# A fourth tile for the weighted values, two tiles for the output, and two steps written in other slices, in a kernel of dilated attention and a binary convolution

## The chip, the core and the metric

The kernel runs on one core of a Trainium2 chip. Its time is the device time of the core in microseconds (us); three runs are given with their median. Besides these there is one profiled execution, whose trace tells when every instruction of every engine started and ended. The engines are called as the profile calls them: PE does the matrix multiplications (PEld is its loading of weights), DVE is VectorE, ACT is ScalarE, POOL is GpSimd, SP is SyncE, which issues most of the DMAs.

## The reference, cut to what matters

The input is an image batch `x` of 16 x 56 x 56 x 384 in float32. There are two layers, each with a residual.

```python
# layer 0: attention over 9 dilated neighbours, three groups of 128 channels
x = x + attention(_gn(x), w_qkv, w_proj, b_proj)
# layer 1: depthwise 3x3 convolution with the signs of w
x = x + conv(_gn(x), sign(clip(w)))

def _gn(v, G=32, eps=1e-5):          # over a whole image and 12 channels
    g = v.reshape(B_, H_, W_, G, C_ // G)
    return (g - mean(g)) / sqrt(var(g) + eps)

def _dilate_attention(q, k, v, head_dim, kernel, dil):   # per group, dil = 1, 2, 3
    attn = einsum('bgdn,bgdkn->bgnk', q, unfold(k)) * head_dim ** -0.5
    attn = softmax(attn, axis=-1)                         # over the 9 neighbours
    return einsum('bgnk,bgdkn->bgnd', attn, unfold(v))
```

Each group has 4 heads of 32 channels, so a pixel has 3 x 4 x 9 = 108 attention weights. The output of layer 0 is projected with `w_proj`.

## The kernel before, in words

Channels lie on the partitions, three groups `j` or `g` of 128. An image is cut into 7 chunks of 8 rows (448 pixels), so there are 112 chunks `m`. The work of all chunks is cut into small pieces; `at(when, order, piece)` files a piece under a slice of time and an order in this slice, and at the end all pieces are emitted in that order. A chunk begins every 9 slices (`STEP = 9`). Written order is not the last word: the framework that builds the program plans each engine's queue itself, from the written order and from when it thinks that inputs and tiles will be there.[...]

What a chunk goes through, with `t0 = 9 m`:

- Stage A (`plan_a`, 12 or more chunks ahead): the pixels are turned so that channels lie on partitions (L423), copied out (L435), `bn_stats` gathers the statistics of layer 0 (L436), and the chunk goes to DRAM.
- Stage B, slices `t0 - 14` to `t0 + 26`: PE projects q, k and v (L464). DVE multiplies q with k for three neighbours at a time into a tile `t` of 128 x 1344 (L517), PE sums over the channels of a head (L502) into the scores `ps`. In slices `t0 + 9` to `t0 + 12` comes the softmax: ACT copies the scores (L534), PE turns them (L537), DVE takes maxima, sums and the quotient (L540 to L548), ACT rounds the weights to bfloat16 (L556), GpSimd subtracts (L560, `softmax_4`), rounds the rest (L564) and subtracts again (L565), so that each weight is three bfloat16 terms. SP then issues a transposing DMA of them into `aT` (L570).
- Weighing (`weigh(i)`, i = 0 to 8, slices `t0 + 14 + i`): PE spreads three neighbours' weights over the channels (L583) into the PSUM tile `pb_a`, of which there is one. DVE multiplies it with v into a tile `w` of 128 x 1344 (L590). In a group of three, with `ky` = 0, 1, 2, GpSimd adds the second and the third `w` to the first (L598, twice) and then sums the three neighbours in it to `y` (L601, L602). PE projects `y` (L616), DVE adds the residual (L619) and gathers the statistics of layer 1 (L622).
- Stage C (`plan_c`, 10 chunks later): two groups are convolved on PE from normalised tiles `z` (L697, L711), the third with ACT's products (L762), which GpSimd adds (L768, L773, L776). PE turns the result (L783), ACT copies it to a tile `osb` (L788), SP issues the DMA to the output (L791). The last image goes other ways: its `z_last` uses tiles of `t` and `w`, its `osb_last` tiles of `y`.

Between images stands `group_norm`, filed by `statistics` as six steps: `channels` (L310, three `bn_aggr` of DVE per set of statistics), `mean`, `deviation`, `variance`, `invert` and `spread_out`, in slices 0, 1, 2, 4, 5 and 7 after `when`. In the middle of the run one call serves layer 1 of image b and layer 0 of image b + 2.

Tiles come from pools. `w_p` has 3 tiles of `w` (L151), `o_p` 3 of `osb` (L158). A pool gives out the tile that has been free for the longest, and an instruction that writes it waits for the last one that used it. With three tiles of `w` this makes the multiplication L590 wait as follows: for `ky` = 0 for the first addition (L598) of the group before, for `ky` = 1 for the second addition of the group before, for `ky` = 2 for its last sum to `y` (L602). A tile `w` goes 5376 bytes into each partition, an `osb` 1536, `rest` 2048.

Of the kernel before, what the change touches and what calls it, by code (L numbers as in the profile page):

```python
# [8 lines left out]
F32 = mybir.dt.float32  # L9
# [8 lines left out]
P = 128  # L18
HEADS = 4
HD = 32  # L20
NG = 3
# [3 lines left out]
SUB = 112  # L25
# [3 lines left out]
NPAD = 32  # L29
# [6 lines left out]
def dilated_attention_then_binary_conv(  # L36
# [28 lines left out]
    nc = tc.nc  # L65
    B, H, W, C = x.shape
    PX = ROWS * W
    NCH = H // ROWS
    NSUB = PX // SUB
# [12 lines left out]
    of = out.rearrange("b h w c -> b (h w) c")  # L82
# [63 lines left out]
    st_p = ctx.enter_context(tc.tile_pool(name="st_p", bufs=2))  # L146
# [1 line left out]
    xn_p = ctx.enter_context(tc.tile_pool(name="xn_p", bufs=3))  # L148
    xr_p = ctx.enter_context(tc.tile_pool(name="xr_p", bufs=1))
    t_p = ctx.enter_context(tc.tile_pool(name="t_p", bufs=4))  # L150
    w_p = ctx.enter_context(tc.tile_pool(name="w_p", bufs=3))  # L151
    y_p = ctx.enter_context(tc.tile_pool(name="y_p", bufs=4))
    s_p = ctx.enter_context(tc.tile_pool(name="s_p", bufs=1))
    a_p = ctx.enter_context(tc.tile_pool(name="a_p", bufs=2))
    x1_p = ctx.enter_context(tc.tile_pool(name="x1_p", bufs=2))
    xg_p = ctx.enter_context(tc.tile_pool(name="xg_p", bufs=2))
    m_p = ctx.enter_context(tc.tile_pool(name="m_p", bufs=3))
    o_p = ctx.enter_context(tc.tile_pool(name="o_p", bufs=3))  # L158


    kv = []
# [134 lines left out]
    def group_norm(sets):  # L296

        had = {}
        L = len(sets)

        def channels():
            had["ch"] = ch = st_p.tile([P, L, NG, 2], F32, tag=f"ch{L}", name="ch")
            for n, (stats, _, _) in enumerate(sets):
                for j in range(NG):
                    nc.vector.bn_aggr(ch[:, n, j, :], stats[:, j].rearrange("p c s -> p (c s)"))  # L310

        def mean():
            had["pair"] = pair = st_p.tile([GN_G, L, 3], F32, tag=f"pair{L}", name="pair")
            pm = ps_mt.tile([P, 512], F32, tag="mt", name="pm")
            for j in range(NG):
                nc.tensor.matmul(
                    pm[:GN_G, 0:L], gsel[:, j], had["ch"][:, :, j, 0], start=(j == 0), stop=(j == NG - 1)
                )
            nc.vector.tensor_scalar_mul(pair[:, :, 2], pm[:GN_G, 0:L], -1.0 / GN_CH)

        def deviation():

            ch = had["ch"]
            pb = ps_mt.tile([P, 512], F32, tag="mt", name="pb")
            for j in range(NG):
                nc.tensor.matmul(
                    pb[:, j * L : (j + 1) * L], gselT[:, j], had["pair"][:, :, 2], start=True, stop=True
                )
            had["dev"] = dev = st_p.tile([P, L, NG], F32, tag=f"dev{L}", name="dev")
            nc.vector.tensor_tensor(  # L330
                dev, pb[:, : NG * L].rearrange("p (j l) -> p l j", l=L), ch[:, :, :, 0], ALU.add
            )
            nc.gpsimd.tensor_tensor(dev, dev, dev, ALU.mult)
            nc.gpsimd.tensor_tensor(dev, dev, ch[:, :, :, 1], ALU.add)

        def variance():
            dev = had["dev"]
            pv = ps_mt.tile([P, 512], F32, tag="mt", name="pv")
            for j in range(NG):
                nc.tensor.matmul(pv[:GN_G, 0:L], gsel[:, j], dev[:, :, j], start=(j == 0), stop=(j == NG - 1))  # L340
            had["var"] = var = st_p.tile([GN_G, 3, L], F32, tag=f"var{L}", name="var")
            v, r = var[:, 0], var[:, 1]
            nc.vector.tensor_scalar(v, pv[:GN_G, 0:L], 1.0 / GN_CH, 1e-5, op0=ALU.mult, op1=ALU.add)

            ri = r.bitcast(I32)
            nc.vector.tensor_single_scalar(ri, v.bitcast(I32), 1, op=ALU.arith_shift_right)
            nc.vector.tensor_scalar(ri, ri, -1, RSQRT_BITS, op0=ALU.mult, op1=ALU.add)

        def invert():

            var, pair = had["var"], had["pair"]
            v, r, t = var[:, 0], var[:, 1], var[:, 2]
            for step in range(3):
                nc.gpsimd.tensor_tensor(t, r, r, ALU.mult)
                nc.gpsimd.tensor_tensor(t, t, v, ALU.mult)
                nc.gpsimd.tensor_scalar(t, t, -0.5, 1.5, op0=ALU.mult, op1=ALU.add)
                nc.gpsimd.tensor_tensor(pair[:, :, 1] if step == 2 else r, r, t, ALU.mult)
            nc.gpsimd.tensor_tensor(pair[:, :, 0], pair[:, :, 2], pair[:, :, 1], ALU.mult)

        def spread_out():  # L360
            pair = had["pair"]
            pp = ps_mt.tile([P, 512], F32, tag="mt", name="pp")
            for j in range(NG):
                nc.tensor.matmul(
                    pp[:, 2 * L * j : 2 * L * (j + 1)], gselT[:, j], pair[:, :, 0:2], start=True, stop=True
                )
            mr = st_p.tile([P, NG, L, 2], F32, tag=f"mr{L}", name="mr", bufs=5 - L)
            nc.vector.tensor_copy(mr.rearrange("p j l s -> p (j l s)"), pp[:, : 2 * L * NG])
            for n, (_, done, for_convolution) in enumerate(sets):
                if not for_convolution:  # L370
                    done(mr[:, :, n])
                    continue

                pz = ps_mt.tile([P, 512], F32, tag="mt", name="pz")
                for s in range(JG * NQ):
                    of_set = gselT[:, s // NQ, s % NQ * HD : s % NQ * HD + HD]
                    for ky in range(3):
                        nc.tensor.matmul(
                            pz[ky * HD : (ky + 1) * HD, 2 * s : 2 * s + 2], of_set, pair[:, n, 0:2],
                            start=True, stop=True,  # L380
                        )
                mrz = st_p.tile([K3, JG, NQ, 2], F32, tag="mrz", name="mrz")
                nc.vector.tensor_copy(mrz.rearrange("p j q s -> p (j q s)"), pz[:K3, : 2 * JG * NQ])
                done(mr[:, :, n], mrz)

        return channels, mean, deviation, variance, invert, spread_out

    def chunk_of(dram, c):
# [4 lines left out]
    def at(when, order, piece):  # L393

        pieces.setdefault((when, order), []).append(piece)

    stats0, stats1 = {}, {}
    xd, x1d = {}, {}
    mr0, mr1 = {}, {}
# [46 lines left out]
    def plan_b(m, t0):  # L446

        b, c = divmod(m, NCH)
        had = {}
# [75 lines left out]
        def by_neighbour(ap):  # L525
            return ap.rearrange("p s (o k) -> p s o k", o=NTAP)

        def over_neighbours(ap):
            return ap.unsqueeze(2).to_broadcast([SUB, NSUB, NTAP, GH])

        def softmax_1():

            sT = s_p.tile([P, PX], F32, tag="sT", name="sT")
            nc.scalar.copy(sT, had.pop("ps")[:, :PX])  # L534
            pt = ps_mt.tile([P, 512], F32, tag="mt", name="pt_s")
            for s in range(NSUB):
                nc.tensor.transpose(pt[:SUB, s * P : (s + 1) * P], sT[:, s * SUB : (s + 1) * SUB], permf)  # L537
            pt4 = pt[:SUB].rearrange("p (s v) -> p s v", s=NSUB)[:, :, :NR]
            mx = s_p.tile([SUB, NSUB, GH], F32, tag="mx", name="mx")
            nc.vector.reduce_max(mx, by_neighbour(pt4).rearrange("p s o k -> p s k o"), axis=AX.X)  # L540
            nc.vector.tensor_tensor(by_neighbour(weights), by_neighbour(pt4), over_neighbours(mx), ALU.subtract)
            nc.scalar.activation(weights, weights, AF.Exp, scale=SCALE)
# [13 lines left out]
            nc.scalar.copy(term[0], e8)  # L556

        def softmax_4():
            had["rest"] = rest = s_p.tile([SUB, NSUB * NPAD * HEADS], F32, tag="rest", name="rest")
            nc.gpsimd.tensor_tensor(rest.rearrange(EIGHTS, k=8), e8, term[0], ALU.subtract)  # L560

        def softmax_5():
# [72 lines left out]
        at(t0 + 9, SOFTMAX, softmax_1)  # L635
        at(t0 + 10, SOFTMAX, softmax_2)
        at(t0 + 11, SOFTMAX, softmax_3)
        at(t0 + 11, PROJECT, softmax_4)
        at(t0 + 12, SOFTMAX, softmax_5)
        at(t0 + 12, LOADS, turn_weights)  # L640
        for i in range(9):
# [182 lines left out]
    SOFTMAX, SCORE, STATISTICS, CONVOLVE, WEIGH, QUERY, SPREAD, QKV, PROJECT, STAGE_A, STAGE_C, NORM, LOADS = range(13)  # L824
# [22 lines left out]
    def statistics(when, sets):  # L847

        steps = {}

        def norm(k):
            if k == 0:
                steps["of"] = group_norm([
                    (stats1.pop(b), lambda mr, mrz, b=b: mr1.update({b: (mr, mrz)}), True) if layer
                    else (stats0.pop(b), lambda mr, b=b: mr0.update({b: mr}), False)
                    for layer, b in sets
                ])
            steps["of"][k]()

        for k in range(6):  # L860
            at(when + STAT_SLICE[k], STAT_ORDER[k], lambda k=k: norm(k))

    for b in range(2):
        statistics(start_a(NCH * b + NCH - 1) + 5, [(0, b)])
# [38 lines left out]
```

## Time and profile before

| what | value |
|---|---|
| time, median of three runs | 5359.44 us (5357.7 to 5360.04) |
| time of the profiled execution | 5363.24 us |
| its span, from the first instruction to the last | 5361.5 us |
| granted clock of PE, mean | 0.978 of full speed |
| busy PE / DVE / POOL / ACT | 5146.8 / 4173.9 / 4254.0 / 2310.0 us |
| L598 (POOL adds w) | 672 instructions, 3080 ns mean |
| L590 (DVE makes w) | 1008 instructions, 1543 ns mean |
| L560, L565 (POOL, rest and third term) | 112 each, 1154 and 1159 ns mean |
| L310 (DVE, aggregation) | 96 instructions, 336 ns mean |
| L788 (ACT, osb) and its DMA | 420, 482 ns median; 3.5 us from issue to landing |

How to read it: the profile has a page with the busy time of each engine, and its trace answers questions: which engine waited how long for what (the waits), what happened in order of time on one engine (the timeline; its columns are start in us, duration in us, engine, line, operation, output and inputs, shapes, count of merged instructions, and in brackets the idle time of the engine just before and what ended it), and busy times and the granted clock in a stretch of time. Idle time of an engine costs something only where the engine that sets the end waits for it in turn.

### The profile page before, as it was taken

Reading aid. Unit: us, or ns where it says so; the run is one execution under the profiler, and the core shown is the slowest. Engines: PE = TensorE matmul, PEld = TensorE weight load, DVE = VectorE, ACT = ScalarE, POOL = GpSimd, SP = SyncE. Lnnn points to the kernel's source line nnn. Section 1 sums busy time; section 2 is a strip of 40 time slices with the busy share of each in tenths; the row PEclk is TensorE's granted clock in tenths of the full one; section 3 lists DMA queues with packets and bytes.
Section 4 is the critical chain, followed back from the end, with each engine's and each line's share of the span. In section 5 each row is a group of like instructions: output and inputs, shape, how many; then the busy total and the mean of one; then the engine's idle time right before and its main releaser. Section 6 shows DMA issues by size and latency. Waiting matters only on the chain. (4 is left out here: it accounts for less than half of the span.)

```text
span 5361.5 us, 75511 instructions
## 1 busy us (share of the span) xinstructions
PE 5146.8 (96%) x26885; PEld 2339.3 (44%) x26885; DVE 4173.9 (78%) x4125; ACT 2310.0 (43%) x4077; POOL 4254.0 (79%) x2950
## 2 busy tenths in 40 slices
PE   8999999999999999999999999999999999999976
PEld 4444444444444444444444444444444444444433
DVE  5887887778778777887878877777887878877764
ACT  3213444444444444444444444444434444444434
POOL 2777888888888887878888888888888888788881
PEclk8999999999999999999999999999999999999986
DMA  6434555555555555555555555565555555544455
GB/s 192 135 108 113 166 161 162 161 155 162 155 164 157 152 159 162 166 155 161 161 154 166 147 161 161 160 165 154 165 158 155 162 147 164 146 135 134 130 135 154
DMA packets 811631, 825.62 MB, mean 154 GB/s; under 512 B 360307, under 2 KB 801014, under 8 KB 811254
## 3 DMA queue, kind: packets, MB, share of 16 engines
q1 hardware_dynamic: 803270, 808.79, 54.7%
q10 hardware_dynamic: 7984, 12.00, 0.7%
q8 instruction: 213, 3.49, 0.3%
q14 instruction: 164, 1.34, 0.1%
HBM read 466.41 MB, written 231.21 MB: 130 GB/s over the span
## 5 line engine op out<-in xcount | busy, mean ns | idle before, releaser
L598 POOL TENSOR_TENSOR w<-w 128x1344 f32<-128x1344 f32 x672 | 2069.9, 3080 | 587.3 <-DVE w L590 544.6
L590 DVE TENSOR_TENSOR w<-pb_a,v 128x1344 f32<-128x1344 f32 x1008 | 1555.7, 1543 | 327.4 <-PE pb_a L583 213.9
L517 DVE TENSOR_TENSOR t<-pq,k 128x1344 f32<-128x1344 f32 x1008 | 1536.2, 1551 | 252.0 <-PE pq L464 251.6
L464 PE MATMUL pkv<-xn,wqkvT 128*128 128x448 f32 x3924 | 1567.6, 548 | 0.4 <-DVE xr L619 0.4
L464 PEld LDWEIGHTS pkv<-xn,wqkvT 128*128 128x128 f32 x3924 | 718.0, 190 | 670.7 <-issue 644.9
L464 PE MATMUL pq<-xn,wqkvT 128*128 128x448 f32 x1962 | 858.8, 573 | 0.0
L616 PE MATMUL po<-y,wprojT 128*128 128x448 f32 x2016 | 832.8, 549 | 23.9 <-POOL y L602 18.4
L697 ACT ACTIVATE z<-z,mrz 96x448 f32<-96x448 f32 x840 | 578.2, 751 | 631.6 <-DMA z<-x1d 371.5
L768 POOL TENSOR_TENSOR m<-m 128x1344 f32<-128x1344 f32 x210 | 640.1, 3048 | 147.4 <-ACT m L762 143.1
L502 PE MATMUL ps<-t,sel 128*32 128x448 f32 x6048 | 663.5, 548 | 45.0 <-DVE t L517 44.3
L762 ACT ACTIVATE m<-zg,ktap 128x448 f32<-128x448 f32 x945 | 555.5, 659 | 8.6 <-POOL xg L776 1.7
L616 PEld LDWEIGHTS po<-y,wprojT 128*128 128x128 f32 x2016 | 375.6, 191 | 381.5 <-issue 339.5
L711 PE MATMUL pc<-z,kdiag 96*32 96x440 f32 (+1 forms) x5040 | 517.5, 544 | 6.1 <-POOL z L699 4.4
L464 PEld LDWEIGHTS pq<-xn,wqkvT 128*128 128x128 f32 x1962 | 353.0, 194 | 330.3 <-issue 330.3
L583 PE MATMUL pb_a<-aT,spread 24*128 24x448 bf16 x3024 | 369.9, 360 | 82.6 <-DMA aT<-e 60.6
L602 POOL TENSOR_TENSOR y<-y,w 128x448 f32<-128x448 f32 x336 | 381.2, 1134 | 16.4
L601 POOL TENSOR_TENSOR y<-w 128x448 f32<-128x448 f32 x336 | 381.3, 1135 | 13.7
L619 DVE SCALAR_TENSOR_TENSOR xr<-po,bias,xr 128x448 f32<-128x448 f32 x336 | 227.9, 678 | 208.5 <-PE po L616 203.8
L474 ACT COPY v<-pkv 128x448 f32<-128x448 f32 x336 | 176.3, 525 | 493.7 <-PE pkv L464 484.7
L718 DVE TENSOR_TENSOR x<-pc,x 128x448 f32<-128x448 f32 x224 | 139.0, 621 | 310.4 <-PE pc L711 309.3
L583 PEld LDWEIGHTS <-spread 24*128 24x128 bf16 x3024 | 100.3, 91 | 571.1 <-issue 488.5
L474 ACT COPY k<-pkv 128x448 f32<-128x448 f32 x336 | 178.9, 532 | 377.2 <-PE pkv L464 377.2
(132 smaller groups left out, 4278.3 us busy)
## 6 DMA issues: line engine op xcount, KB each, us to landing
z<-x1d SPq DMA_DIRECT2D x570, 224.0 KB, 3.8
xr<-xd SPq DMA_DIRECT2D x112, 672.0 KB, 4.2
x1d<-xr SPq DMA_DIRECT2D x112, 672.0 KB, 3.2
xn<-xd SPq DMA_DIRECT2D x109, 672.0 KB, 4.6
xin<-in_x_dram SPq DMA_DIRECT2D x105, 672.0 KB, 7.2
xd<-xa SPq DMA_DIRECT2D x315, 224.0 KB, 3.3
out_dram<-osb SPq DMA_DIRECT2D x420, 168.0 KB, 3.5
x<-x1d SPq DMA_DIRECT2D x112, 448.0 KB, 8.1
```

Source lines behind the costliest of these rows:

```text
L464: nc.tensor.matmul(dst[:, :PX], wqkvT[:, cc, o0 : o0 + P], had["xn"][:, cc, :], start=(cc == 0), stop=(cc == NG - 1))
L502: return nc.tensor.matmul(had["ps"][32 * j : 32 * j + 32, :PX], sel[:, s0 : s0 + 32], tk, start=(issued[j] == 1), stop=(issued[j] == len(r ...
L517: nc.vector.tensor_tensor(t.rearrange("p k (r w) -> p k r w", w=W), q3, k3, ALU.mult)
L583: return nc.tensor.matmul(pb[:, kx, :PX].rearrange("p (s n) -> p s n", s=NSUB), spread[rows_of, v % 2, :], had["a"][rows_of, :, v // 8, :] ...
L590: nc.vector.tensor_tensor(w.rearrange("p k (r w) -> p k r w", w=W), pb[:, :, :PX].rearrange("p k (r w) -> p k r w", w=W), three(kv[1][g][m ...
L598: nc.gpsimd.tensor_tensor(w0, w0, w, ALU.add)
L601: nc.gpsimd.tensor_tensor(y, w0[:, 0], w0[:, 1], ALU.add)
L616: nc.tensor.matmul(po[:, :PX], wprojT[:, g, j * P : (j + 1) * P], had[f"y{g}"], start=(g == 0), stop=(g == NG - 1))
L697: nc.scalar.activation(z, z, AF.Identity, bias=mrz[:, j, q, 0:1], scale=mrz[:, j, q, 1:2])
L711: return nc.tensor.matmul(pcr[q * HD : (q + 1) * HD, :, lo:hi], kdiag[:, kx, j * NQ + q, :], rows(set_of(j, q))[:, :, lo + kx - 1 : hi + k ...
L762: nc.scalar.activation(rows(t[:, kx]), zp[:, ky : ky + ROWS, kx : kx + W], AF.Copy, scale=ktap[:, o : o + 1])
L768: nc.gpsimd.tensor_tensor(had["m"], had["m"], t, ALU.add)
```

## The change

It does these things:

- `w_p` gets four tiles in place of three, `o_p` two in place of three. `rest` no longer has a tile of its own but shares that of `sT`, which is widened from 448 to 512 columns.
- `softmax_4`, GpSimd's subtraction, is filed under `SOFTMAX`, the first order in slice `t0 + 11`, in place of `PROJECT`, which comes after the additions of weighing and convolution.
- `channels` becomes one `bn_aggr` per call. Where a call of `group_norm` has two sets, the three of the second set (layer 0) are filed 3, 2 and 1 slices ahead of `when`; all others stay in slice `when`.

```diff
-    w_p = ctx.enter_context(tc.tile_pool(name="w_p", bufs=3))
+    w_p = ctx.enter_context(tc.tile_pool(name="w_p", bufs=4))
...
-    o_p = ctx.enter_context(tc.tile_pool(name="o_p", bufs=3))
+    o_p = ctx.enter_context(tc.tile_pool(name="o_p", bufs=2))
...
-        def channels():
-            had["ch"] = ch = st_p.tile([P, L, NG, 2], F32, tag=f"ch{L}", name="ch")
-            for n, (stats, _, _) in enumerate(sets):
-                for j in range(NG):
-                    nc.vector.bn_aggr(ch[:, n, j, :], stats[:, j].rearrange("p c s -> p (c s)"))
+        def channels(n, j):
+            if "ch" not in had:
+                had["ch"] = st_p.tile([P, L, NG, 2], F32, tag=f"ch{L}", name="ch")
+            nc.vector.bn_aggr(had["ch"][:, n, j, :], sets[n][0][:, j].rearrange("p c s -> p (c s)"))
...
-            sT = s_p.tile([P, PX], F32, tag="sT", name="sT")
+            sT = s_p.tile([P, NSUB * NPAD * HEADS], F32, tag="sT", name="sT")[:, :PX]
...
-            had["rest"] = rest = s_p.tile([SUB, NSUB * NPAD * HEADS], F32, tag="rest", name="rest")
+            had["rest"] = rest = s_p.tile([P, NSUB * NPAD * HEADS], F32, tag="sT", name="rest")[:SUB]
...
-        at(t0 + 11, PROJECT, softmax_4)
+        at(t0 + 11, SOFTMAX, softmax_4)
...
-        def norm(k):
-            if k == 0:
+        def norm(k, *which):
+            if not steps:
                 steps["of"] = group_norm([
-                    (stats1.pop(b), lambda mr, mrz, b=b: mr1.update({b: (mr, mrz)}), True) if layer
-                    else (stats0.pop(b), lambda mr, b=b: mr0.update({b: mr}), False)
+                    (stats1[b], lambda mr, mrz, b=b: mr1.update({b: (mr, mrz)}), True) if layer
+                    else (stats0[b], lambda mr, b=b: mr0.update({b: mr}), False)
                     for layer, b in sets
                 ])
-            steps["of"][k]()
-
-        for k in range(6):
+            steps["of"][k](*which)
+
+        for n, (layer, _) in enumerate(sets):
+            for j in range(NG):
+                sooner = 3 - j if n and not layer else 0
+                at(when - sooner, STATISTICS, lambda n=n, j=j: norm(0, n, j))
+        for k in range(1, 6):
             at(when + STAT_SLICE[k], STAT_ORDER[k], lambda k=k: norm(k))
```

## The prediction, made before the changed kernel was run

> **What bounds the kernel now.** I read the busy times first: PE is busy for 5146.8 of 5361.5 us, so the end is set by PE's work and by the 215 us in which PE stands still. Next come PE's waits (time in total, how often, longest), since only what shortens these can shorten the run:
>
> ```profile
> PE pb_a L583 <- DMA aT<-e: 60.6, 21, 4.0
> PE ps L502 <- DVE t L517: 44.3, 51, 1.7
> PE pb_a L583 <- DVE w L590: 21.4, 21, 4.1
> PE po L616 <- POOL y L602: 18.4, 3, 10.0
> ```
>
> The reader is to see that 44.3 + 21.4 = 65.7 us are waits for DVE. DVE is busy for only 78%, so it must be held up itself. The view of the tile `w` says by what:
>
> ```profile
> its engine sat idle before it (us, times) until:
>   DVE w L590: 544.6, 313
>   PE pb_a L583: 213.9, 133
>   POOL w L598: 79.2, 47
> ```
>
> The last line matters: 47 times DVE stood before L590 until GpSimd had ended an addition, though the product needs no result of GpSimd. It waited for the tile. The timelines of DVE, PE and POOL around 1990 us show one case whole:
>
> ```profile
> 1991.18 0.59 DVE L541 TENSOR_TENSOR ew<-pt_s,mx 112x432 f32<-112x432 f32 x1
> 1993.70 1.56 DVE L590 TENSOR_TENSOR w<-pb_a,v 128x1344 f32<-128x1344 f32 x1 [1.93 <-POOL w L598]
> 1995.18 0.91 DVE L546 TENSOR_REDUCE sm<-ew 112x48 f32<-112x432 f32 x1
> 1996.00 1.55 DVE L517 TENSOR_TENSOR t<-pq,k 128x1344 f32<-128x1344 f32 x1
> ```
>
> ```profile
> 1995.32 0.37 PE L583 MATMUL pb_a<-aT,spread 24*128 24x448 bf16 x3 [0.34 <-DVE w L590]
> ...
> 1997.61 1.71 PE L502 MATMUL ps<-t,sel 128*32 128x448 f32 x16 [1.45 <-DVE t L517]
> ```
>
> ```profile
> 1980.96 3.06 POOL L598 TENSOR_TENSOR w<-w 128x1344 f32<-128x1344 f32 x1
> ...
> 1990.63 3.04 POOL L598 TENSOR_TENSOR w<-w 128x1344 f32<-128x1344 f32 x1
> ```
>
> GpSimd is late: between its two additions stand 6.5 us of the convolution. Its second one ends at 1993.67, and 0.03 us later DVE begins. Behind L590 in DVE's queue stand L546 and L517; so PE waits 0.34 us to overwrite the only `pb_a`, then 1.45 us for `t`.
>
> **The change, part by part.**
>
> *Fourth tile of w.* Each L590 now needs the release one step earlier in the row (first addition, second addition, last sum to `y`): here the addition that ended at 1984.02 in place of 1993.67. PE's input `pb_a` was ready at 1989.56 and DVE free at 1991.78, so DVE would start 1.9 us sooner. I went through all 1008 L590 like this: in 43 the old release came last, 68.4 us together, and in every one the new release came before the other two conditions. Then for each of them I took the waits of PE for `w` or `t` in the 6 us behind it, but no more than DVE gains. From 600 to 5150 us there are 36 such DVE waits with 44.7 us, and PE gets back 39.4 us of it. Most lie in two neighbouring chunks per image (here 1.79 us at 1993.7, 1.07 us at 2039.6). Before 600 us: 0.29 us at 192.5, 0.82 us at 486.4, 2.42 us at 496.0, together 3.5 us.
>
> Is the gain given back at the next wait? The 3.9 us for `aT`, once per image, follow some 65 us later. That chain starts at a product that waits for PE (at 2081.3), and GpSimd stands idle in between (3.40 us before 2074.5, 2.33 us before 2082.5, 2.18 us before 2088.0), so its backlog of under 2 us is gone; these waits move with PE and stay as long. The other deadlines have room: `aT` lands 2.7 us ahead of its use in the chunk behind the first of the two waits and 3.9 us behind the second; `y` is there 6.1 us ahead of L616. Each loses at most 1.8 us.
>
> *The clock.* After short stalls close together PE runs at half clock for a while. The busy times of a stretch behind the pair of waits at 2690.0 and 2692.3 (0.39 and 1.17 us) end with PE's clock, the DMA share and GB/s:
>
> ```profile
> 2692.30:2695.50 3.20, 3.20 (x20) 0.96 (x24) 2.80 (x5) 0.39 (x1) 2.77 (x2) 0.50 0.54 196
> ```
>
> The Trainium skill (TensorE: Matmul & The Clock Gate, section "Why this matters for your kernels") has it that the clock is kept as long as no gap between matmuls exceeds about 3 us. By that rule gaps of 1.6 us cost nothing beyond themselves. The row shows 0.50, and a row decides. The same 3.4 us at half clock stand at 2692, 3989 and 4638 us, each behind such a pair, and at 497 us behind the 2.42 us wait: 4 x 3.4 x 0.5 = 6.8 us; by the rule 0. The half clock behind the `aT` waits lasts 3.4 or 6.8 us, as it falls; it may come out 5 us either way.
>
> *What the sooner product meets.* A rule speaks against the gain: by the Trainium skill (Advanced Engine Details and Errata, section "GPSIMD Details") GpSimd shares a read and a write interface with DVE and conflicts with DVE instructions that have two inputs in SBUF. L590 has one in PSUM; L548 (`ew` times `sm`) has two. The trace agrees: L548 takes 0.60 us when GpSimd is idle, as at 1999.8, and while an addition runs
>
> ```profile
> 2092.41 2.10 DVE L548 TENSOR_TENSOR ew<-ew,sm 112x432 f32<-112x432 f32 x1
> ```
>
> it ends only about 0.45 us behind that addition (POOL's L768 ends at 2094.05). Moved 1.9 us forward, L548 would begin at 1997.9 under an addition that ends at 1999.1: about 1.65 us in place of 0.60. DVE has 1.00 us idle just behind it (waiting for PE's `pc`), PE's `pc` comes 1.8 us sooner, and L548 still ends 0.8 us sooner than before: the loss at PE is 0.04 us. Without the rule the gain is 39.4; with the cover gone, 1.05 us in each of some 28 places would take 29 us of it. I take nothing, and keep 29 as the far end.
>
> *Two tiles of osb.* ACT's L788 must now wait for the output DMA of two copies ago. Set against the landings (3.5 us from issue, about 0.45 us from copy to issue), 2 of 420 copies would have started too early, by 3.3 us together, both in the last 160 us. The nearest regular case is one copy per image with 0.3 to 1.8 us to spare. ACT is 43% busy; behind L788 in its queue stand copies of k, v and `xa`, which PE would feel only after some us. Cost: 0, at most 5.
>
> *rest in sT's tile.* ACT's next L534 now waits for GpSimd's L565 of the chunk before: the nearest case has 17.3 us to spare. L560 must come behind the turning of `sT` (8.6 us to spare). Cost: 0.
>
> *The two moved steps.* Laying the compiled queues of the two kernels side by side, I find every engine's instructions in the same order up to the last 150 us; only some ten places there are swapped. The planner had already put L560 between two sums of `y`, and spread layer 0's `bn_aggr`. So L560 (1.15 us) and L310 (0.34 us) are issued where they were, pass nothing, and issue no DMA. Gain 0, cost 0.
>
> *The tail, behind 5150 us.* DVE waits four times for tiles (12.8 us), PE 6.3 us behind them. But GpSimd is itself the limit there: from 5156 to 5244 us it idles 2.01 + 0.71 + 1.08 = 3.8 us, and PE stands 10.0 and 7.7 us for its `y`. So 0 to 4 us; with swapped instructions perhaps -3. I take 0.
>
> Sum: 39.4 + 3.5 + 6.8 = 49.7 us. Span 5361.5 - 49.7 = 5311.8 us; the profiled execution took 5363.2 us, the median of the runs 5359.4 us. From the median: **5310 us**, 0.93% less. The likeliest case's own range is 5300 to 5322.
>
> **The rivals.**
>
> *A. Half the gain.* The port conflict or GpSimd's backlog takes part back: L548 costs 29 us (above), or the backlog of up to 2 us reaches `aT`. For: GpSimd is 79% busy, and the chain to `aT` has no idle POOL in its last 17.7 us. Against: the idle times before it. About 5359 - 21 to -29: 5330 to 5338 us.
>
> *B. No change.* PE's waits move elsewhere altogether: 5359 us. For it speaks only that both moves do nothing; against it, that in ordinary chunks PE has no wait at all, so there is no next limit close by.
>
> *C. Slower: the port conflict outweighs the tile.* L548 has been as long as 2.61 us. If the shift put it under an addition in the two chunks and in the one behind them (48 places) and PE stood for all of the 2.0 us, that is 96 us against 49.7 us: 5406 us. It decides from 49.7 / 48 = 1.04 us per place on. Against: DVE's slack and its sooner start.
>
> *D. The moves do what they say,* and GpSimd's subtraction runs right behind ACT's cast (at 2095.2 in place of 2100.7), so that part of the 3.9 us and its half clock vanish: some 12 x 4 = 48 us more, 5262 us. Against: the compiled order.
>
> **How the numbers follow.** Main case 0.64, A 0.20, B 0.06, C 0.06, D 0.04. The range takes 5298 to 5337: nearly the whole main case and about two thirds of A. 0.2% (11 us), which is about what a measurement of this kernel can tell from no change, lies at 5349 and 5370. Faster: main, A and D, 0.88; same: B and the nearest part of C, 0.07; slower: the rest of C, 0.05.
>
> **What would show it.** In the changed kernel L590's idle time for "POOL w" falls from 79.2 us to under 15; PE's waits for `t` and `w` from 65.7 to some 20; PE's wait for `aT` stays near 60 us with the same 3.9 us per image; no half clock near the two chunks in front. L548 lengthens in the chunks with a former wait. If L560 stands earlier in POOL's queue, the moves are not idle and D counts; if PE's wait for `aT` or `y` grows by what the others lose, A or B. The prediction is wrong if the queues on the chip differ from those that I compared, or if the sooner product costs DVE more than its slack.

## The result: 5318.0 us, and the profile after

The changed kernel takes 5318.0 us (median; 5314.2 to 5320.5), the kernel before 5359.7 us in the same comparison: a ratio of 0.9921, 95% interval 0.9904 to 0.9938. The forecast was 5310 us, with 5298 to 5337 for the range. The profiled execution took 5318.4 us, its span is 5316.7 us. (From L310 on, a line of the changed kernel has a number one lower than before: L590 is now L589.)

PE's waits in the profile after (time in total, how often, longest) stand against the four lines shown of before:

```profile
PE pb_a L582 <- DMA aT<-e: 60.4, 20, 4.0
PE po L615 <- POOL y L601: 32.4, 6, 12.3
...
PE pb_a L582 <- DVE w L589: 11.3, 7, 2.0
PE po L615 <- ACT v L473: 9.4, 16, 1.0
...
PE ps L501 <- DVE t L516: 6.9, 19, 1.6
```

The waits for DVE went from 44.3 + 21.4 = 65.7 us to 11.3 + 6.9 = 18.2 us. The wait for `aT` is what it was. Two waits grew: for `y` from 18.4 to 32.4 us, and for ACT's copy of `v` from 5.2 to 9.4 us. The view of the tile `w` fits the expected cause of the first change: DVE hardly waits for GpSimd's release of a tile any more (79.2 us, 47 times, before):

```profile
its engine sat idle before it (us, times) until:
  DVE w L589: 500.8, 262
  PE pb_a L582: 235.8, 140
...
  POOL w L597: 5.7, 5
```

The case of the forecast, at 1993.70 us before, lies at 1980.29 us now. DVE's, PE's and POOL's timelines of the changed kernel:

```profile
1979.78 0.59 DVE L540 TENSOR_TENSOR ew<-pt_s,mx 112x432 f32<-112x432 f32 x1
1980.29 1.55 DVE L589 TENSOR_TENSOR w<-pb_a,v 128x1344 f32<-128x1344 f32 x1
...
1982.57 1.55 DVE L516 TENSOR_TENSOR t<-pq,k 128x1344 f32<-128x1344 f32 x1
```

```profile
1983.51 0.36 PE L582 MATMUL pb_a<-aT,spread 24*128 24x448 bf16 x3
...
1984.27 1.71 PE L501 MATMUL ps<-t,sel 128*32 128x448 f32 x16
```

```profile
1979.23 3.05 POOL L597 TENSOR_TENSOR w<-w 128x1344 f32<-128x1344 f32 x1
```

L589 follows L540 at once, 2.0 us before the addition that it used to wait for ends (1982.28), and PE's 0.34 and 1.45 us in front of the `pb_a` and `ps` matmuls are gone.

Where the time came from is seen best by stretches of the run. The marks are PE's first product of the attention in images 2, 3, 15 and 16 and in the last chunk. Three executions with three tiles of `w` (before, and the runs e1 and e3 below) stand against two with four (the changed kernel and e2); the times are us, from the timelines:

| stretch | three tiles | mean | four tiles | mean | gain |
|---|---|---|---|---|---|
| start to image 2 | 398.5, 401.8, 398.6 | 399.6 | 400.5, 396.9 | 398.7 | 0.9 |
| image 2 | 319.8, 320.0, 320.0 | 319.9 | 316.0, 316.0 | 316.0 | 3.9 |
| images 3 to 14 | 3891.0, 3885.9, 3892.4 | 3889.8 | 3851.7, 3855.0 | 3853.4 | 36.4 |
| image 15 | 316.0, 315.7, 311.8 | 314.5 | 312.0, 311.9 | 312.0 | 2.5 |
| image 16 to its last chunk | 265.3, 266.2, 267.3 | 266.3 | 267.0, 266.9 | 267.0 | -0.7 |
| the end | 171.0, 170.6, 168.3 | 170.0 | 169.5, 168.9 | 169.2 | 0.8 |

The sum is 43.8 us, and 42.8 us of it are earned in images 2 to 15.

### The profile page after: what moved, and what is told of

Read it like the earlier page. It is cut to its first block, busy times and chain, and to the rows that moved or that the text cites. A ratio compares the mean times of both kernels' runs of the same rounds, so it can differ in the third digit from the quotient of the medians.

```text
span 5316.7 us, 75544 instructions
## 1 busy us (share of the span) xinstructions
PE 5131.6 (97%) x26885; PEld 2336.1 (44%) x26885; DVE 4206.7 (79%) x4125; ACT 2310.1 (43%) x4077; POOL 4255.0 (80%) x2950
## 5 line engine op out<-in xcount | busy, mean ns | idle before, releaser
L589 DVE TENSOR_TENSOR w<-pb_a,v 128x1344 f32<-128x1344 f32 x1008 | 1555.3, 1543 | 274.0 <-PE pb_a L582 235.8
L615 PE MATMUL po<-y,wprojT 128*128 128x448 f32 x2016 | 835.2, 551 | 41.8 <-POOL y L601 32.4
L582 PE MATMUL pb_a<-aT,spread 24*128 24x448 bf16 x3024 | 369.6, 360 | 71.7 <-DMA aT<-e 60.4
L601 POOL TENSOR_TENSOR y<-y,w 128x448 f32<-128x448 f32 x336 | 381.6, 1136 | 16.3
L600 POOL TENSOR_TENSOR y<-w 128x448 f32<-128x448 f32 x336 | 381.4, 1135 | 13.6
```

The source lines that it names most:

```text
L582: return nc.tensor.matmul(pb[:, kx, :PX].rearrange("p (s n) -> p s n", s=NSUB), spread[rows_of, v % 2, :], had["a"][rows_of, :, v // 8, :] ...
L589: nc.vector.tensor_tensor(w.rearrange("p k (r w) -> p k r w", w=W), pb[:, :, :PX].rearrange("p k (r w) -> p k r w", w=W), three(kv[1][g][m ...
L601: nc.gpsimd.tensor_tensor(y, y, w0[:, 2], ALU.add)
L615: nc.tensor.matmul(po[:, :PX], wprojT[:, g, j * P : (j + 1) * P], had[f"y{g}"], start=(g == 0), stop=(g == NG - 1))
```

## The experiments

### e1 and e2: the moves alone, the tile alone

e1 is the kernel before with the two moved steps and nothing else. e2 is the kernel before with the pools alone:

```diff
-    w_p = ctx.enter_context(tc.tile_pool(name="w_p", bufs=3))
+    w_p = ctx.enter_context(tc.tile_pool(name="w_p", bufs=4))
...
-    o_p = ctx.enter_context(tc.tile_pool(name="o_p", bufs=3))
+    o_p = ctx.enter_context(tc.tile_pool(name="o_p", bufs=2))
...
-            had["rest"] = rest = s_p.tile([SUB, NSUB * NPAD * HEADS], F32, tag="rest", name="rest")
+            had["rest"] = rest = s_p.tile([P, NSUB * NPAD * HEADS], F32, tag="sT", name="rest")[:SUB]
```

Expected of e1:

> The kernel before with the two moved steps alone: softmax_4 in the SOFTMAX place of its slice and one bn_aggr of layer 0 in each of the three slices ahead; w_p 3, o_p 3, rest in a tile of its own. My theory (the moves are idle, since every engine's compiled order is the same up to the last 150 us): 5359 us, ratio 0.999 to 1.001, PE's wait for aT 60 us and DVE's wait for POOL w 79 us as before. Rival D (the moves act): the 12 waits of 3.9 us for aT and their half clock get shorter, 5310 to 5320 us, and the fourth tile would then be worth nothing.

Expected of e2:

> The kernel before with the pools alone: w_p 4, paid for by o_p 2 and rest in sT's tile; the steps stay where they were. My theory: all of the gain, 5318 us like the changed kernel (0.992), DVE's wait for POOL w about 6 us in place of 79. Rival D: about 5359 us.

Measured: e1 5357.6 us beside 5357.2 us of the kernel before, ratio 0.9998 (0.9990 to 1.0007). e2 5315.0 us, 0.9920 (0.9906 to 0.9933). In e1's tile view DVE waits nearly as in the kernel before (79.2 us, 47 times there):

```profile
  POOL w L597: 70.6, 42
```

So the moves do nothing, and the pools do everything. Rival D, as the change is written, is out.

### e3: what the space costs

The changed kernel with `w_p` at 3; the two tiles of `osb`, the shared tile and the moves stay.

> The changed kernel with w_p back at 3; two tiles of osb, rest in sT's tile and the moves stay. It shows what the space costs. My theory: 0, that is 5359 us (0.999 to 1.001) and DVE's wait for POOL w 79 us; if the two osb tiles or the shared tile hold ACT or GpSimd up, up to 5 us more, 5364 us, and part of the 8 us that my forecast missed would lie there.

Measured: 5360.2 us, ratio 1.0008 (1.0000 to 1.0016), so between 0 and 9 us, most likely about 4. With three tiles a small cost of the space can't be excluded. With four it isn't seen: in the changed kernel ACT waits three times for an output DMA before it writes an `osb`, 4.0 us in all (the prediction had two copies and 3.3 us), and PE waits 0.5 us for ACT's copies to `osb`, as it did before.

### e4: the subtraction really moved (rival D made true)

In the changed kernel the steps from ACT's cast on are planned one or two slices sooner, and GpSimd's first sum to `y` of that slice is ordered behind them by hand:

```diff
-        at(t0 + 11, SOFTMAX, softmax_3)
-        at(t0 + 11, SOFTMAX, softmax_4)
-        at(t0 + 12, SOFTMAX, softmax_5)
-        at(t0 + 12, LOADS, turn_weights)
+        at(t0 + 10, SOFTMAX, softmax_3)
+        at(t0 + 10, SOFTMAX, softmax_4)
+        at(t0 + 10, SOFTMAX, softmax_5)
+        at(t0 + 10, LOADS, turn_weights)
...
+            ahead["of_y"] = nc.gpsimd.tensor_tensor(term[2], r8, term[1], ALU.subtract)
...
+                first_sum = nc.gpsimd.tensor_tensor(y, w0[:, 0], w0[:, 1], ALU.add)
+                if i == 5 and "of_y" in ahead:
+                    tc.add_manual_dep(
+                        first_sum.ins, ahead.pop("of_y").ins.name,
+                        mybir.DependencyInfo(mybir.DependencyClass.NoSync, mybir.DependencyReason.DATA),
+                        reason="subtraction ahead of the sums",
+                    )
```

> The changed kernel with GpSimd's three instructions on the exponentials (rest, its cast, the second difference) really moved: all steps from the cast on planned one or two slices sooner, and the first sum to y of that slice ordered behind them on GpSimd's queue. In the chunk of the long aT wait this takes two sums to y (1.14 us each) and the convolution's sum to xg (1.15 us) out of the chain to aT, about 3.3 us. Theory (that queue order is what sets the 3.9 us): PE's wait for aT falls from 60 to about 20 us, 12 x 3.3 = 40 us less, 5278 us, and down to 5255 us if the half clock behind these waits goes too. Rival (something else is late next, or y, now about 3 us later in every chunk, becomes PE's wait): the wait for y grows by what the wait for aT loses, 5310 to 5325 us.

Measured: 5263.7 us, ratio 0.9825 (0.9812 to 0.9838), 54 us faster than the changed kernel (51 us by the two ratios). PE's wait for `aT` fell from 60.4 to 26.6 us:

```profile
PE pb_a L583 <- DMA aT<-e: 26.6, 15, 2.4
```

POOL's timelines of the chunk with the long wait, first the changed kernel, then e4:

```profile
2085.12 1.14 POOL L772 TENSOR_TENSOR m<-m 128x448 f32<-128x448 f32 x1
2086.21 1.14 POOL L600 TENSOR_TENSOR y<-w 128x448 f32<-128x448 f32 x1
2087.31 1.17 POOL L559 TENSOR_TENSOR rest<-ew,e 112x512 f32<-112x512 f32 x1
2088.43 1.14 POOL L601 TENSOR_TENSOR y<-y,w 128x448 f32<-128x448 f32 x1
2089.51 0.61 POOL L563 CAST e<-rest 112x512 bf16<-112x512 f32 x1
2090.08 1.15 POOL L775 TENSOR_TENSOR xg<-m,xg 128x448 f32<-128x448 f32 x1
2091.18 1.17 POOL L564 TENSOR_TENSOR e<-rest,e 112x512 bf16<-112x512 f32 x1
```

```profile
2060.57 1.13 POOL L779 TENSOR_TENSOR m<-m 128x448 f32<-128x448 f32 x1
2061.66 1.15 POOL L560 TENSOR_TENSOR rest<-ew,e 112x512 f32<-112x512 f32 x1
2062.77 1.13 POOL L782 TENSOR_TENSOR xg<-m,xg 128x448 f32<-128x448 f32 x1
2063.86 0.60 POOL L564 CAST e<-rest 112x512 bf16<-112x512 f32 x1
2064.54 1.16 POOL L565 TENSOR_TENSOR e<-rest,e 112x512 bf16<-112x512 f32 x1
2065.66 1.14 POOL L601 TENSOR_TENSOR y<-w 128x448 f32<-128x448 f32 x1
```

In the changed kernel four sums stand before or between the three instructions, though the cast that they wait for had ended at 2081.83. In e4 the two sums to `y` are behind them; the convolution's two (L779, L782) are not. So each wait lost about 2 us (3.93 to 1.86 us here), not the 3.3 us that I expected.

By stretches the 54 us come out like this. Images 3 to 14 gained 40 us (3851.7 to 3811.4): the waits for `aT` fell from 47.2 to 22.8 us and the loss at half clock (half of the time at half clock) from 27.3 to 1.7 us, while PE's wait for `v` rose from 7.7 to 14.1 us. Another 11 us came ahead of image 2 (400.5 to 389.3), where the waits for `aT` fell from 9.7 to 0.4 us. The busy times behind the wait end with PE's clock, the DMA share and GB/s, first in the changed kernel, then in e4:

```profile
2095.00:2099.00 4.00, 2.60 (x6) 1.28 (x7) 1.56 (x1) 0.00 (x0) 3.84 (x3) 0.67 1.05 226
```

```profile
2068.00:2072.00 4.00, 2.22 (x8) 1.16 (x9) 1.56 (x1) 0.00 (x0) 3.92 (x3) 1.00 1.04 266
```

In images 3 to 14 of these two executions PE runs at half clock behind the waits of 3.9 us, and not behind those of 1.8 to 2.4 us. That the length of the wait is the cause is not shown: in e5 waits as short as these are followed by it. Between 330 and 5000 us the loss at half clock is 32.4 us in the changed kernel and 6.8 us in e4, which is 25.6 us less. The total lies between the expected 5278 and 5255 us partly by luck: images 3 to 14 gave less from the waits than expected, and the gain ahead of image 2 was not in the sum.

### e5: is the tile still worth its price then?

e4 with `w_p` at 3, every queue in the same order.

> The kernel with GpSimd's three instructions moved ahead, with w_p back at 3; every engine's compiled order stays the same. Theory (the fourth tile removes waits of its own, which have nothing to do with the wait for aT): the 40 us of PE's waits for DVE and the half clock behind them come back, 40 to 50 us slower than with four tiles (5263.7), so 5304 to 5314 us. Rival (the moved instructions also end GpSimd's lateness, so that the tile is worth little): 5265 to 5280 us.

Measured: 5284.8 us, ratio 0.9865 (0.9848 to 0.9881): the tile is worth 21 us here, not the 42 us of e2 against e1. My expectation failed, and so did the rival's; it lies in between. PE's two waits for DVE in e5:

```profile
PE pb_a L583 <- DVE w L590: 20.7, 9, 4.4
PE ps L502 <- DVE t L517: 20.7, 35, 1.7
```

That is 41.4 us in place of 61.1 us in e1 (20.8 + 40.3): with the three instructions ahead, the pairs of waits in two neighbouring chunks are gone and one of about 1 us per image, at another place, is left. So the order of GpSimd's queue and the fourth tile cure partly the same lateness. Why the pairs go I have not tested.

Against e4, PE's waits for DVE are 25.3 us longer (16.1 us there) and the loss at half clock between 330 and 5000 us is 10.3 us larger (17.1 against 6.8 us); shorter waits for `y` and `v` give 16.3 us back. In 7 of images 3 to 14 half clock stands at a wait for `aT` of 1.8 to 2.4 us, where e4 has waits of the same length and none of it.

### e6: the convolution's sums out of the way too

As e4, but the first sum to `y` of every group, and all sums of the convolution to `m` and `xg`, are ordered behind the latest of the three instructions that was planned ahead of them:

```diff
+    def behind_subtraction(first):
+        last = ahead.get("last")
+        if last is not None:
+            tc.add_manual_dep(
+                first.ins, last.ins.name,
+                mybir.DependencyInfo(mybir.DependencyClass.NoSync, mybir.DependencyReason.DATA),
+                reason="behind the subtraction",
+            )
...
-                nc.gpsimd.tensor_tensor(t[:, 0], t[:, 0], t[:, kx], ALU.add)
+                behind_subtraction(nc.gpsimd.tensor_tensor(t[:, 0], t[:, 0], t[:, kx], ALU.add))
...
-                nc.gpsimd.tensor_tensor(mid, t[:, 0], mid, ALU.add)
+                behind_subtraction(nc.gpsimd.tensor_tensor(mid, t[:, 0], mid, ALU.add))
```

> As the kernel with the three instructions moved ahead, and the convolution's sums (to m and to xg) ordered behind them too, which takes another 1.13 + 1.13 us out of the chain to aT. Theory: the 1.86 us that are left of the wait for aT, once per image, go: 12 x 1.86 = 22 us less than 5263.7, about 5241 us; half clock has little left to give (6.8 us between 330 and 5000 us). Rival (PE's next limit stands close behind, or the convolution's output comes late): 5255 to 5270 us.

Measured: 5241.2 us, ratio 0.9783 (0.9768 to 0.9797), the expected number. The 1.86 us per image are gone. A new wait for GpSimd's part of the group norm stands in their place, 15 times and at most 1.0 us:

```profile
PE pv L339 <- POOL dev L333: 13.3, 15, 1.0
```

So the number is partly luck: images 3 to 14 gained 13.8 us (3811.4 to 3797.6) and not 22, and other stretches made up for it, most of all the one from image 16 to its last chunk (266.7 to 260.5).

### e7: the sums of the last two chunks on DVE

On top of e6, the two sums to `y` of the last two chunks go to DVE:

```diff
+                sums = nc.vector if m >= N - 2 else nc.gpsimd
+                first_sum = sums.tensor_tensor(y, w0[:, 0], w0[:, 1], ALU.add)
...
+                sums.tensor_tensor(y, y, w0[:, 2], ALU.add)
```

> As the one before, with the sums to y of the last two chunks on DVE. It tests why the fourth tile gained nothing behind 5150 us: theory, GpSimd is itself the limit there (PE waits 7.1, 8.2 and 12.3 us for y), so 12 sums of 1.13 us taken off its queue bring 8 to 14 us at the end, about 5230 us if the run before gives 5241. Rival (DVE or the normalisation behind the last y sets the end): 0 to 4 us.

Measured: 5251.6 us, ratio 0.9802 (0.9788 to 0.9817), 10 us slower than e6. Both theories missed it. DVE's timeline shows what went wrong:

```profile
5051.66 0.62 DVE L612 TENSOR_TENSOR y<-w 128x448 f32<-128x448 f32 x1 [5.08 <-POOL w L608]
...
5083.74 3.42 DVE L612 TENSOR_TENSOR y<-w 128x448 f32<-128x448 f32 x1 [4.49 <-POOL w L608]
```

The sum needs GpSimd's addition. DVE stands 5.08 us before it, and the next product L600, for which PE's `pb_a` had been ready since 5044.68, begins only behind it, at 5053.26. PE then waits 5.34 us for `w` at 5054.9, and GpSimd itself 6.52 us at 5058.65. Besides, a sum with two inputs in SBUF took up to 3.42 us where it takes 0.62 us alone.

### e8: the price of the port conflict

The changed kernel with another second multiplication in the softmax; the division by the sum is left out:

```diff
-            nc.vector.tensor_tensor(by_neighbour(weights), by_neighbour(weights), over_neighbours(sm), ALU.mult)
+            nc.vector.tensor_scalar(by_neighbour(weights), by_neighbour(weights), 0.125, None, op0=ALU.mult)
```

> The changed kernel, with the second multiplication of the softmax (L547, ew times sm, both in SBUF) replaced by a multiplication with a constant, so that it has one input in SBUF; the division by the sum is left out. GpSimd's cast-side instructions come a little sooner in its queue by this, so the wait for aT can change by itself; what counts is L547's time and PE's waits for DVE. Theory (the longer L547 is hidden behind DVE's idle time): L547 falls from 131 us to 60 us or less whatever GpSimd does, and PE's waits for t and w stay at 18 us within 4. Rival A (the conflict costs up to 29 us): these waits fall by 10 us or more, or the kernel gains more than the wait for aT explains.

Measured: 5321.6 us, ratio 0.9933 (0.9919 to 0.9948). The instruction did not get shorter: its times (minimum, median, maximum in ns) and PE's wait for DVE were

```profile
L547 DVE TENSOR_SCALAR ew<-ew x112: 308/1958/3145, 104.8 to 5129.6; 112x432 f32<-112x432 f32 x112
```

```profile
PE pb_a L582 <- DVE w L589: 42.3, 56, 1.7
```

So with one input in SBUF it is held as well: 0.31 us alone, 1.96 us in the median, and both expectations failed. DVE's and POOL's timelines, and then PE's, show one case:

```profile
1943.94 3.15 DVE L547 TENSOR_SCALAR ew<-ew 112x432 f32<-112x432 f32 x1
1947.01 1.54 DVE L589 TENSOR_TENSOR w<-pb_a,v 128x1344 f32<-128x1344 f32 x1
```

```profile
1943.80 3.04 POOL L597 TENSOR_TENSOR w<-w 128x1344 f32<-128x1344 f32 x1
```

```profile
1948.60 0.37 PE L582 MATMUL pb_a<-aT,spread 24*128 24x448 bf16 x3 [1.37 <-DVE w L589]
```

But e8 is no clean measure of the price, since this edit also changed the order of all four engines' queues. In the changed kernel L547 stands just behind a product L589 in 108 of 112 chunks; in e8 it stands just in front of one in 110. What holds L547 there holds the next product too, and PE with it. Counting what L547 takes above its time alone (0.60 us, 0.33 us in e8), it is held 64 us in the changed kernel (46 places), 25 us before (16 places) and 146 us in e8 (80 places). PE's waits for DVE within 5 us of the start of a held one are 4.5 us in the changed kernel, 1.3 us before and 35 us in e8. How much of the 35 us comes from the longer holding and how much from the place in the queue is not shown. The wait for `aT` fell to 11.3 us, since the three instructions too stand sooner in GpSimd's queue; PE's waits for DVE (51.1 us against 18.2) and for `v` (23.8 us against 9.4) took that gain back.

### e9 to e12: the last chunk again

e9 puts the last chunk's additions and sums on DVE together, so that DVE has nothing of GpSimd to wait for; e10 does so for the last channel group of that chunk only. Both are on top of e6. The edit of e10 (in e9 the condition is `m == N - 1` alone, and in both the two sums go the same way):

```diff
+            adder = nc.vector if m == N - 1 and g == NG - 1 else nc.gpsimd
+            adder.tensor_tensor(w0, w0, w, ALU.add)
```

Expected of e9:

> The fastest kernel so far (three instructions and the convolution's sums reordered, 5241.2 us) with both the additions of w and the sums to y of the last chunk on DVE, so that DVE no longer waits in its queue for GpSimd's additions as it did when only the sums moved. GpSimd loses 6 additions of 3.05 us and 6 sums of 1.13 us. Theory (GpSimd's queue is what PE's last waits for y stand on, and the last attempt failed by DVE's waiting for GpSimd between them): PE's last wait for y, 12.75 us, goes down to some 4 us, 6 to 12 us less, 5230 to 5235 us. Rival (two inputs in SBUF: each DVE addition is held until GpSimd's instruction ends, 1.5 us become 3 or more, and the products behind them are late): 5240 to 5250 us.

Expected of e10:

> As the run beside it, but with the additions and sums of the last chunk's last channel group alone on DVE: 2 additions and 2 sums leave GpSimd's queue. PE's order stays as it was. Theory: GpSimd's 2 x 3.05 + 2 x 1.13 = 8.4 us in front of the last projection become 2 x 1.55 + 2 x 0.62 = 4.3 us on DVE, beside GpSimd's convolution: 4 to 8 us less, about 5235 us. Rival (the additions are held by the convolution's additions on GpSimd): 5239 to 5246 us.

Measured: e9 5240.1 us, 0.9769 (0.9752 to 0.9785); e10 5235.6 us, 0.9767 (0.9753 to 0.9782). These intervals reach into e6's (e9 lies where its rival had it), so e6 and e10 were run once more side by side.

Expected of e11, which is e6:

> The kernel with the three instructions and the convolution's sums reordered once more, beside the next one on the same chip, since the two lie within each other's spread so far. Both theories: 5236 to 5243 us.

Expected of e12, which is e10:

> The same with the last channel group of the last chunk on DVE. Theory (GpSimd's queue is what the last y stands on): 4 to 7 us less than the kernel beside it, as in the first comparison, with intervals that no longer overlap by much. Rival (chance): within 2 us of it.

Measured: e11 5238.4 us, 0.9775 (0.9762 to 0.9789); e12 5237.5 us, 0.9770 (0.9756 to 0.9783). So e10 is no faster than e6 by anything that these runs can tell, which is what the rival of e12 said. PE's last wait for `y` did fall, from 12.75 us in e6 to 6.29 us in e10. In e10 DVE's additions cost more than thought, as DVE's and POOL's timelines show:

```profile
5100.22 4.10 DVE L609 TENSOR_TENSOR w<-w 128x1344 f32<-128x1344 f32 x1
```

```profile
5099.89 7.31 POOL L781 TENSOR_TENSOR m<-m 128x1344 f32<-128x1344 f32 x2
```

The addition takes 4.10 us in place of 1.55 us, and GpSimd's two take 7.31 us where they took 6.11 us in e7: both engines pay. In e12, the same kernel, DVE's two additions took 1.56 and 2.06 us, and the last wait for `y` was 6.20 us against 12.32 us in e11. Why so little of that reaches the end stays open.

The fastest kernels of the study are e6 and e10, at about 5238 us: 2.3% less than before, 1.5% less than the changed kernel.

## Why the prediction was right, and what it missed

*The fourth tile: right, in place and size.* The waits for POOL's release went (79.2 to 5.7 us), and e2 alone has all of the gain. Over images 3 to 15 the profiled pair gained 39.3 + 4.0 = 43.3 us; my steps put 36.8 us of waits (39.4 us less 1.1 in image 2 and 1.5 in image 16) and 5.1 us of clock, 41.9 us, into that stretch. But inside that sum two errors nearly cancel. The clock gave 8.5 us, as told below. Against it stands a wait that I had not foreseen: the copy of `v` (over images 3 to 14 from 3.1 to 7.7 us, where PE's waits for `t` and `w`, 34.8 us before, are gone). I had looked at ACT only for `osb`, and called it 43% busy. The two tiles of `osb` are not the cause: e3 has them, with three tiles of `w`, and PE waits 2.4 us for `v` there; e2, with four, has 7.9 us. ACT's and PE's timelines of the changed kernel show how it comes:

```profile
2008.53 4.04 ACT L761 ACTIVATE m<-zg,ktap 128x448 f32<-128x448 f32 x7
2012.47 0.51 ACT L473 COPY v<-pkv 128x448 f32<-128x448 f32 x1
```

```profile
2013.04 2.15 PE L615 MATMUL po<-y,wprojT 128*128 128x448 f32 x5 [1.02 <-ACT v L473]
```

Seven operations of the convolution stand in ACT's queue ahead of the copy that makes PE's accumulator free. PE, no longer held by DVE, comes to it 1.0 us too soon: the next engine in line takes a share of the gain.

*The clock: right in size, not in place.* The profiled pair lost 8.5 us less at half clock over images 3 to 15, where I had 5.1 us; for the place at 497 us I had the other 1.7 us, and half clock stands there still. The row of before was one execution's: over the three profiled executions with three tiles the loss between 330 and 5000 us is 42.7, 41.0 and 42.7 us, over the two with four 32.4 and 39.3 us, so 6.3 us in the mean, with 6.9 us between the last two. The granted clocks of all executions bear the size out: the loss over the whole span is 109.0 us in the mean of the 25 executions of before that ran beside e2, and 101.0 us in e2's five. The place shown before (2692.30 us) lies near 2670 us now, and nothing is lost there; a row of the changed kernel, with the clock of 1.00 ahead of the DMA share:

```profile
2640.00:2700.00 60.00, 60.00 (x325) 27.70 (x318) 51.45 (x53) 22.03 (x39) 50.15 (x45) 1.00 0.70 183
```

The rule of the Trainium skill (TensorE: Matmul & The Clock Gate, section "Why this matters for your kernels"), by which only gaps of over about 3 us cost clock, is not what the runs show: in e1 half clock stands at 2001 and 4267 us, as it does before at 2692 us, with no wait of over 2 us near (0.32 and 1.45 us at both places in e1). Nor does the length of one wait decide: in e4 the waits of 1.83 to 2.41 us for `aT` in images 3 to 14 were followed by none, those of 1.73 and 1.72 us in images 15 and 16 by one each, and in e5 7 of 12 waits of 1.81 to 2.39 us by one. What does decide stays open.

*The port conflict: right.* L547 lengthened where its product had waited, from 92.0 to 131.4 us in all. In images 3 to 14 it takes 1.0 to 1.9 us in the first of the two chunks and 2.1 to 2.2 us in the second, in place of 0.60 us. The case of the forecast, on DVE before, then on DVE and POOL in the changed kernel:

```profile
1999.76 0.60 DVE L548 TENSOR_TENSOR ew<-ew,sm 112x432 f32<-112x432 f32 x1
```

```profile
1986.33 1.88 DVE L547 TENSOR_TENSOR ew<-ew,sm 112x432 f32<-112x432 f32 x1
```

```profile
1984.67 6.43 POOL L597 TENSOR_TENSOR w<-w 128x1344 f32<-128x1344 f32 x2
```

This is the conflict that the Trainium skill names (Advanced Engine Details and Errata, section "GPSIMD Details") for two inputs in SBUF. The first of the two additions ends at 1987.74 and L547 at 1988.21, 0.47 us behind it; I had estimated 1.65 us. PE paid no more than 4.5 us behind such places, so the forecast's nothing was near, and its far end of 29 us far. In e8 L547 stands in front of the product, and PE waited 35 us behind it. So rival C's mechanism is real; here it lacked the place in the queue or the size, and the runs don't tell which. e8's idea, that one input in SBUF keeps clear of GpSimd, had left out half of that page's sentence, which names instructions in a 2-port mode as well; whether e8's L547 ran in such a mode no run here shows.

*The two moved steps: right* (e1). In the traces the instructions of PE, DVE, ACT and GpSimd stand in the same order before and after the change up to 5150 us, and in e1 in the order of before to the end. *Two tiles of osb, rest in sT's tile:* no cost that the four-tile runs show, 0 to 9 us by e3. *The wait for `aT`: right*, 60.4 us and 3.93 us per image. *Rival D:* its condition was false, as said, but its price was near: 48 us forecast for the 12 images, 40 us measured there in e4.

*The 8 us that were missed.* The profiled pair differs by 5363.2 - 5318.4 = 44.8 us, the sum had 49.7 us. Three terms fall 6.2 us short, and images 3 to 15 gave 1.4 us more than their steps:
- "Before 600 us", image 2: PE's wait of 2.42 us at 496.0 us went, but a wait for `y` of 2.09 us stands at 501.7 us instead, with the half clock still behind it. I had counted both as gain: 6.0 us in this image (3.2 and 1.1 us of waits, 1.7 us of clock) against 3.8 us measured, 2.2 us short.
- Image 16 and the end: my steps had 1.5 us of steady waits up to 5150 us and then "I take 0". The pair lost 1.7 us and gained 1.5 us there, 1.7 us short. A wait of 1.23 us for `t` (5132.9 us before) is now one of 1.96 us for `w` (5090.3 us). Behind it DVE's waits for tiles turned into waits for `y`, 18.4 to 32.4 us, as the step's reason said. But that GpSimd alone is the limit there is not shown: e7 to e12 took work off it, and nothing came of it that these runs can tell.
- The start: forecast 0.3 us, measured 2.0 us more (one more half clock). In e2 it took 1.6 us less than before, so this is chance.

The other 3.4 us are the way to the median: the profiled execution of before ran 3.8 us above its median and that of the changed kernel 0.4 us, and I took a sum from the one off the other.

## What to carry to other kernels

When an engine waits for a buffer and not for data, a further tile gives the wait back, but count behind it: the same lead makes the consumer arrive early at the next engine's queue (here ACT's), and at the end of the run, where the consumer waits for the releasing engine's results too, it gave nothing here. Before you add a tile, look at the order of the late engine's queue: three instructions moved ahead of sums brought more (54 us) than the tile (42 us), and behind that move the tile was worth 21 us. About half of the 54 us was clock. Work that is moved to another engine's queue holds up what stands behind it there while it waits (5.08 us in e7). And a change of one instruction can change the order of every queue, as in e8: compare the orders before you read a cause from the time.

## What the runs showed of the hardware

- While GpSimd works, a DVE multiplication with a constant and one SBUF input (112 x 432, float) is held as well: 0.31 us alone, 1.96 us in the median, 3.1 us at most; the one with two inputs takes 0.60 us alone, and up to 2.2 us in images 3 to 14 (3.1 us at most, at 5085.6 us of the changed kernel). It ends about 0.24 us (one input) or 0.4 to 0.5 us (two) after GpSimd's instruction.
- The conflict works in both directions where both have long additions: 1.55 to 4.10 us on DVE, 6.11 to 7.31 us for two on GpSimd.
- A wait of 3.9 us came with PE's half clock for 3.4 or 6.8 us in each of 12 images; with shorter waits it came sometimes and sometimes not (waits of 1.8 to 2.4 us: 0 of 12 in e4, 7 of 12 in e5).
